# Turning half of a transformer's ternary stages by DMA: six stages on one core, groups 3 to 15 as two 16-bit planes, Gelu in PSUM, second-half tiles among first-half products

## The chip, the core and the metric

The kernel runs on 1 core of one Trainium2 chip. The metric is the device time of one execution in microseconds (us). Three runs of the kernel before the change gave 2587.43, 2589.55 and 2590.55; the median is 2589.55. A difference below about 0.2% (5 us) can't be told from no change.

The engines are named as the profile names them: PE is TensorE (matrix products), PEld its weight loads, DVE is VectorE, ACT is ScalarE, POOL is GpSimd, SP is SyncE, which issues most of the DMAs.

## What is computed

The input x is 8 x 1024 rows of 256 numbers (float32). Six stages follow, each with a residual:

```python
x = x + 0.5 * fp4_ffn(layernorm(x))
x = x + decay_attention(layernorm(x))
x = x + 0.5 * fp4_ffn(layernorm(x))
x = x + 0.5 * ternary_ffn(layernorm(x))
x = x + memory_attention(layernorm(x))
x = x + 0.5 * ternary_ffn(layernorm(x))
```

The change is in the two ternary stages. With W1 (1024 x 256) and W2 (256 x 1024) rounded to -1, 0, 1, one computes

```python
h = gelu(einsum('bsd,fd->bsf', x, ternary(W1)) + b1)
out = einsum('bsf,df->bsd', h, ternary(W2)) + b2
```

## The kernel before

x stays in SBUF for the whole program, as 16 groups `X[g]` of 512 rows: 128 partitions (rows of a tile) x 4 tiles x 256. NG is 16, G is 4 (tiles per group), NF is 8 (blocks of 128 hidden numbers), P is 128, TG is 512.

The program is written in Python through a library that sets all semaphores, hands out buffers and orders each engine's instructions at compile time: it takes the instructions of the text in their order and moves one forward when the earlier ones are not ready by its own model of times. `pin` ties instructions to their written order in other stages; in the ternary stages (`loose`) it does not. A pool with `bufs=n` hands out n buffers per tag in turn, and a buffer is free when all its users are done.

`ffn_ternary` (L1138) runs a loop of 18 turns (L1237). In turn g:

- `norm_turn(g)` (L1168 on) turns the normalized group g from rows to columns. For each of the two halves of the 256 numbers, four 128x128 transposes on TensorE against the identity (L1174) fill a PSUM bank `pt`; ScalarE casts it to a rounded 32-bit type, `xh` (L1177), and VectorE subtracts that from the bank, `xl` (L1179), so that xh + xl carries the full precision through two products.
- `hidden(g - 1)` makes the first half of the feed-forward for the group before: for each f of 8 blocks, four products of 128x512 (L1193) into a PSUM bank `ph`, Gelu on ScalarE from `ph` to the SBUF tile `hf` (L1201), a rounded copy `hh` on ScalarE (L1202), and the remainder `hl` = hf - hh on VectorE (L1204). Behind the first blocks stand the entries of `between`: the normalization of group g + 1 (`norm`, four VectorE operations, L1155), a share of the LayerNorm statistics (`ln.advance`: L235, L236 and small Newton steps L248 to L264), and in the last turns the begin of the next stage. Behind the last four blocks stand the additions of the second bias (`biased`, L1165).
- `down(g - 2)` makes the second half: for each of four tiles, 16 products of 128x256 (L1220) into a bank `po`, and VectorE adds half of it to `X[g]` (L1228). In the last stage the finished group is written to the output by a DMA on SP's queue (L1235; the last group tile by tile, L1233).

PSUM has eight banks here: 2 for `pt`, 4 for `ph`, 2 for `po`. `hf` has four buffers, `hh` and `hl` two each.

How far ahead the statistics are made is a plan (L353): sizes of the pieces in groups, and for each group the turn by which it is due.

The program already turns data by DMA elsewhere: in the fp4 stages a `dma_start_transpose` moves 16-bit grids (L912, L1084), from SP's queue.

Of the kernel before, what the change touches and what calls it, by code (L numbers as in the profile page):

```python
# [9 lines left out]
F32 = mybir.dt.float32  # L10
F32R = mybir.dt.float32r
BF16 = mybir.dt.bfloat16
I32 = mybir.dt.int32
AF = mybir.ActivationFunctionType
ALU = mybir.AluOpType
AX = mybir.AxisListType
PSUM = bass.MemoryType.PSUM

P = 128
D = 256  # L20
# [3 lines left out]
G = 4  # L24
TG = G * P
# [14 lines left out]
def macaron_kernel(  # L40
# [25 lines left out]
    nc = tc.nc  # L66
    NB, S, _ = x.shape
    NG = NB * S // TG
# [16 lines left out]
    out_v = out.rearrange("b s d -> (b s) d").rearrange("(g t p) d -> g p t d", t=G, p=P)  # L85
# [4 lines left out]
    xn_pool = ctx.enter_context(tc.tile_pool(name="xn_pool", bufs=1))  # L90
# [38 lines left out]
    X = []  # L129
    for g in range(NG):  # L130
        xg = xpool.tile([P, G, D], F32, name=f"x_{g}")
        X.append(xg)
        if g == 0:
# [4 lines left out]
                out=A0.lng[:, H : H + 2], in_=gamma_rep.rearrange("(m p) -> p m", p=P)  # L138
# [11 lines left out]
    b1c = w_l1.tile([P, NF], F32, name="b1c")  # L150
# [117 lines left out]
    def statistics(sizes, dues):  # L268
# [81 lines left out]
        "fp4": ((3, 1, 2, 4, 4, 2), [0 if g < 3 else G * (g - 2) + 2 for g in range(NG)]),  # L350

        "decay": ((2, 2, 4, 4, 4), [max(0, G * g - 5) for g in range(NG)]),
        "ternary": ((2, 2, 4, 4, 4), [max(0, g - 1) for g in range(NG)]),  # L353

        "memory": (
            (GB + 3, 3, 4, NG), [max(0, G * (g - GB) - 4) for g in range(NG)]
# [42 lines left out]
    def transpose_group(src, dst, psum, tag, both_act=False, pin=lambda ins: ins):  # L399

        for k in range(2):
            pt = psum.tile([P, TG], F32, tag=tag, name="pt")
            for j in range(G):
                pin(
                    nc.tensor.transpose(
                        pt[:, j * P : (j + 1) * P], src[:, j, k * P : (k + 1) * P], ident
                    )
                )
            if k == 0 or both_act:
                nc.scalar.copy(dst[:, k, :], pt)  # L410
            else:
                pin(nc.vector.tensor_copy(dst[:, k, :], pt))

    def fp4_first(xn, mg, pool):

# [722 lines left out]
    def ffn_ternary(last, after=None):  # L1138
        with ExitStack() as st:
            lnp = st.enter_context(tc.tile_pool(name="f1_ln", bufs=2))  # L1140
            hp = st.enter_context(tc.tile_pool(name="f1_h", bufs=2))
            tp = st.enter_context(tc.tile_pool(name="f1_t", bufs=4))
            ps_t = st.enter_context(tc.tile_pool(name="f1_pt", bufs=2, space=PSUM))
            ps_h = st.enter_context(tc.tile_pool(name="f1_ph", bufs=4, space=PSUM))
            ps_o = st.enter_context(tc.tile_pool(name="f1_po", bufs=2, space=PSUM))
            xns, xts, hs = {}, {}, {}
            ln, xns[0] = begun.pop("ternary")
            loose.append("ternary")

            def norm(g):  # L1150
                xn = xn_pool.tile([P, G, D], F32, tag="xn", name="xn")
                for j in range(G):
                    n = G * g + j
                    pin(
                        nc.vector.tensor_scalar(  # L1155
                            xn[:, j, :], X[g][:, j, :], ln.mv[:, n, 0:1], ln.lr[:, n : n + 1],
                            ALU.subtract, ALU.mult,
                        )
                    )
                xns[g] = xn  # L1160

            def biased(j, g):

                xj = X[g][:, j, :]
                pin(nc.vector.tensor_tensor(xj, xj, b2h, ALU.add))  # L1165

            def norm_turn(g):
                xn = xns.pop(g)  # L1168
                xh = lnp.tile([P, 2, TG], F32R, tag="xh", name="xh")
                xl = lnp.tile([P, 2, TG], F32R, tag="xl", name="xl")  # L1170
                for k in range(2):
                    pt = ps_t.tile([P, TG], F32, tag="pt", name="pt")
                    for j in range(G):
                        nc.tensor.transpose(  # L1174
                            pt[:, j * P : (j + 1) * P], xn[:, j, k * P : (k + 1) * P], ident
                        )
                    nc.scalar.copy(xh[:, k, :], pt)  # L1177
                    pin(
                        nc.vector.tensor_tensor(  # L1179
                            xl[:, k, :], pt, xh[:, k, :].bitcast(F32), ALU.subtract  # L1180
                        )
                    )
                xts[g] = (xh, xl)

            def hidden(g, between):
                xh, xl = xts.pop(g)
                hh = hp.tile([P, NF, TG], F32R, tag="hh", name="hh")
                hl = hp.tile([P, NF, TG], F32R, tag="hl", name="hl")
                for f in range(NF):
                    ph = ps_h.tile([P, TG], F32, tag="ph", name="ph")  # L1190
                    for k in range(2):
                        for xt in (xh, xl):
                            nc.tensor.matmul(  # L1193
                                ph,
                                lhsT=w1[:, k, f * P : (f + 1) * P],
                                rhs=xt[:, k, :],
                                start=(k == 0 and xt is xh),
                                stop=(k == 1 and xt is xl),
                            )
                    hf = tp.tile([P, TG], F32, tag="hf", name="hf")  # L1200
                    nc.scalar.activation(hf, ph, AF.Gelu, bias=b1c[:, f : f + 1])  # L1201
                    nc.scalar.copy(hh[:, f, :], hf)  # L1202
                    pin(
                        nc.vector.tensor_tensor(  # L1204
                            hl[:, f, :], hf, hh[:, f, :].bitcast(F32), ALU.subtract
                        )
                    )
                    if f < len(between):
                        between[f]()
                    elif f >= NF - G:  # L1210
                        biased(f - NF + G, g)
                hs[g] = (hh, hl)

            def down(g):
                hh, hl = hs.pop(g)
                for j in range(G):
                    po = ps_o.tile([P, D], F32, tag="po", name="po")
                    for f in range(NF):
                        for ht in (hh, hl):
                            nc.tensor.matmul(  # L1220
                                po,
                                lhsT=ht[:, f, j * P : (j + 1) * P],
                                rhs=w2[:, f, :],
                                start=(f == 0 and ht is hh),
                                stop=(f == NF - 1 and ht is hl),
                            )
# [7 lines left out]
                if last and g < NG - 1:  # L1234
                    nc.sync.dma_start(out=out_v[g], in_=X[g])  # L1235

            for g in range(NG + 2):  # L1237
                between = []
                if g < NG:
                    norm_turn(g)  # L1240
                    if g + 1 < NG:
                        between.append(lambda: norm(g + 1))
                    between.append(lambda: ln.advance(g))
                    if after and g >= NG - 6:
                        between.append(lambda: begin(after, NG - g))
                if 0 <= g - 1 < NG:
                    hidden(g - 1, between)
                else:
                    for do in between:
                        do()  # L1250
                if 0 <= g - 2 < NG:
                    down(g - 2)
            loose.pop()


# [850 lines left out]
```

## Time and profile before

The profile is of one execution on the chip.

| What | us |
|---|---|
| profiled execution | 2594.43 |
| its span, first to last instruction | 2592.7 |
| median of three runs | 2589.55 |
| first ternary stage, first L1193 to last L1220 | 1491.8 to 1748.4 |
| second ternary stage, the same | 2332.5 to 2589.3 |

The granted TensorE clock is 0.993 over the span and 1.00 in all stretches of the ternary stages.

| Row (line, engine, tile) | count | mean ns of one |
|---|---|---|
| L1174 PE, transposes to pt | 256 | 278 |
| L1193 PE, first half, ph | 1024 | 398 |
| L1220 PE, second half, po | 2048 | 280 |
| L1201 ACT, Gelu | 256 | 695 |
| L1202 ACT, hh | 256 | 628 |
| L1204 DVE, hl | 256 | 684 |
| L1177 ACT, xh | 64 | 590 |
| L1179 DVE, xl | 64 | 680 |
| L1155 DVE, normalization | 120 | 407 |
| L1165 DVE, bias addition | 128 | 415 |
| L1228 DVE, tile addition | 128 | 421 |
| L1486 POOL, 128x1024 addition (another stage) | 16 | 2385 |

How to read it: a TensorE product overlaps the next, so its mean is longer than its share of the time, and distances between starts are used instead. In lists of instructions, "x8" merges eight of a kind, and a bracket at the end tells how long the engine had been idle before the line and what released it. Times in them are us from the span's start.

### The profile page before, as it was taken

How to read it: one execution, taken by the hardware profiler on the slowest of the kernel's cores; microseconds unless marked ns; L12 is line 12 of the kernel's file. 1: busy time of each engine (PE TensorE's matmuls, PEld its weight loads, DVE VectorE, ACT ScalarE, POOL GpSimd, SP SyncE). 2: the span in 40 equal slices, each digit the busy share in tenths (PEclk: the TensorE clock that was granted, in tenths of full speed). 3: DMA queues.
4: the chain of work that ended last, by engine and by line, in shares of the span. 5: the costliest groups of instructions: out<-in, count | busy, mean ns of one | idle time of the engine just before them, and what ended most of it. 6: DMA issues, size and time to landing. Idle time of an engine off the chain costs nothing.

```text
span 2592.7 us, 52415 instructions
## 1 busy us (share of the span) xinstructions
PE 2506.9 (97%) x20426; PEld 1868.6 (72%) x20426; DVE 2087.8 (81%) x4808; ACT 1235.1 (48%) x2785; POOL 900.9 (35%) x895
## 2 busy tenths in 40 slices
PE   4899999999999999999999999999999999999999
PEld 2577777766666666777777689995677776778998
DVE  7898888758878778988888599647888888879864
ACT  5344444334333333444444276656555555437664
POOL 4565555521101003555555300004555555530000
PEclk9899999999999999999999999999999999999999
DMA  7455556500000002556555300000000000000001
GB/s 218 87 117 115 113 118 116 107 23 18 10 22 14 2 2 48 114 116 115 117 116 113 66 1 1 1 1 1 2 2 2 2 2 2 2 2 26 33 33 41
DMA packets 199897, 132.40 MB, mean 51 GB/s; under 512 B 138048, under 2 KB 174944, under 8 KB 199648
## 3 DMA queue, kind: packets, MB, share of 16 engines
q1 hardware_dynamic: 198704, 127.85, 22.8%
q8 instruction: 161, 2.64, 0.4%
q0 software_dynamic: 240, 0.54, 0.1%
q14 instruction: 88, 0.72, 0.1%
q10 hardware_dynamic: 704, 0.66, 0.1%
HBM read 80.77 MB, written 16.52 MB: 38 GB/s over the span
## 4 chain that ended last, share of the span: by engine, by line
PE 84%; DVE 11%; ACT 2%; issue 1%; DMA 1%; POOL 1%; SPq 0%; DVEq 0%; POOLq 0%; ACTq 0%
PE po L960 11%; PE pu L861 10%; PE pg L861 10%; PE po L1220 9%; PE ph L1193 9%; PE sc L1263 5%; PE py L1347 5%; PE pq L1361 4%; PE pkv L1361 4%; PE po L1361 4%; PE pk L1361 4%; PE py L1329 2%; PE pmo L1786 2%; DVE at L1272 1%; DVE qp L804 1%
## 5 line engine op out<-in xcount | busy, mean ns | idle before, releaser
L960 PE MATMUL po<-wd,ht 128*128 128x256 f32 x1536 | 358.1, 383 | 0.6 <-DVE x L969 0.5
L861 PE MATMUL pu<-wgu,xt 128*128 128x352 f32 x1024 | 349.6, 464 | 8.3 <-DVE h L876 7.9
L861 PE MATMUL pg<-wgu,xt 128*128 128x352 f32 x1024 | 348.8, 463 | 4.4 <-ACT sg L871 4.1
L960 PEld LDWEIGHTS po<-wd,ht 128*128 128x128 f32 x1536 | 294.6, 193 | 62.4 <-issue 2.2
L871 ACT ACTIVATE sg<-pg 128x352 f32<-128x352 f32 x256 | 118.1, 461 | 451.5 <-PE pg L861 422.6
L817 POOL TENSOR_TENSOR h<-h,q_rs 128x704 f32<-128x704 f32 (+1 forms) x128 | 176.2, 1376 | 413.1 <-DVE q_rs L811 413.1
L861 PEld LDWEIGHTS pu<-wgu,xt 128*128 128x128 f32 x1024 | 186.5, 193 | 112.3 <-issue 19.6
L861 PEld LDWEIGHTS pg<-wgu,xt 128*128 128x128 f32 x1024 | 195.0, 191 | 97.8 <-ACT sg L871 9.2
L1220 PE MATMUL po<-w,hl 128*128 128x256 f32 x1024 | 243.7, 280 | 1.4 <-DVE hl L1204 1.2
L1220 PE MATMUL po<-w,hh 128*128 128x256 f32 x1024 | 243.3, 280 | 0.0
L1902 POOL TENSOR_TENSOR mo<-mo 128x256 f32<-128x256 f32 x192 | 164.2, 855 | 196.6 <-DVE mo L1799 188.1
L927 POOL TENSOR_TENSOR ht<-gt,ht 128x768 f32<-128x768 bf16 x124 | 205.7, 1659 | 0.0
L1193 PE MATMUL ph<-xh,w 128*128 128x512 f32 x512 | 204.4, 401 | 1.4 <-ACT hf L1201 0.6
L1193 PE MATMUL ph<-xl,w 128*128 128x512 f32 x512 | 201.8, 395 | 0.0
L1204 DVE TENSOR_TENSOR hl<-hf,hh 128x512 fp32r<-128x512 f32 x256 | 168.3, 684 | 39.4 <-ACT hh L1202 35.9
L1220 PEld LDWEIGHTS po<-w,hl 128*128 128x128 f32 x1024 | 192.1, 188 | 4.5 <-DVE hl L1204 2.5
L1220 PEld LDWEIGHTS po<-w,hh 128*128 128x128 f32 x1024 | 192.1, 188 | 2.6 <-DVE x L1228 0.3
L1201 ACT ACTIVATE hf<-ph,b1c 128x512 f32<-128x512 f32 x256 | 168.0, 695 | 18.5 <-PE ph L1193 16.1
L1272 DVE TENSOR_TENSOR at<-sc,dec 128x512 f32<-128x512 f32 x256 | 158.6, 682 | 11.8 <-PE sc L1263 11.8
L886 DVE SCALAR_TENSOR_TENSOR h<-qp,h 128x704 f32<-128x704 f32 x124 | 110.2, 889 | 69.1 <-ACT qp L821 68.9
L1272 DVE TENSOR_TENSOR at<-sc,tri 128x512 f32<-128x512 f32 x256 | 164.9, 679 | 0.4 <-PE sc L1263 0.4
L1202 ACT CAST hh<-hf 128x512 fp32r<-128x512 f32 x256 | 149.2, 628 | 17.0 <-PE po L1220 15.2
(276 smaller groups left out, 5303.0 us busy)
## 6 DMA issues: line engine op xcount, KB each, us to landing
ht<-sd SPq DMA_DIRECT2D x124, 384.0 KB
xt<-sd SPq DMA_DIRECT2D x56, 256.0 KB
sd<-sct SPq DMA_DIRECT2D x124, 64.0 KB
x<-in_x SPq DMA_DIRECT2D x15, 512.0 KB
out<-x SPq DMA_DIRECT2D x15, 512.0 KB
t_raw<-in_w_t SPq DMA_DIRECT2D x16, 256.0 KB
gt<-gd SPq DMA_TRANSPOSE x124
gtx<-xn SPq DMA_TRANSPOSE x56
```

What stands on the lines that cost most here:

```text
L817: pin(mul.tensor_tensor(vb, vb, rs[:, :, None].to_broadcast([P, nb, 16]), ALU.mult))
L861: nc.tensor.matmul(ps, lhsT=xts[g][:, 2 * j + k, :], rhs=wgu[:, k, (2 * q + of_up) * NHALF : (2 * q + of_up + 1) * NHALF], start=(k == 0), ...
L927: nc.gpsimd.tensor_tensor(wide.rearrange("p c t -> p (c t)"), grid.rearrange("p c t -> p (c t)"), wide.rearrange("p c t -> p (c t)"), ALU. ...
L960: nc.tensor.matmul(po, lhsT=ht[:kn, c, :], rhs=wd[:kn, c, :], start=(c == 0), stop=(c == NC - 1),)
L1193: nc.tensor.matmul(ph, lhsT=w1[:, k, f * P : (f + 1) * P], rhs=xt[:, k, :], start=(k == 0 and xt is xh), stop=(k == 1 and xt is xl),)
L1201: nc.scalar.activation(hf, ph, AF.Gelu, bias=b1c[:, f : f + 1])
L1202: nc.scalar.copy(hh[:, f, :], hf)
L1204: nc.vector.tensor_tensor(hl[:, f, :], hf, hh[:, f, :].bitcast(F32), ALU.subtract)
L1220: nc.tensor.matmul(po, lhsT=ht[:, f, j * P : (j + 1) * P], rhs=w2[:, f, :], start=(f == 0 and ht is hh), stop=(f == NF - 1 and ht is hl),)
L1272: nc.vector.tensor_tensor(at, sc.rearrange("p m (e t) -> p (m e) t", e=2), weight, ALU.mult)
L1361: nc.tensor.matmul(dst, lhsT=lhsT, rhs=rhs, start=n == 0, stop=n == len(parts) - 1)
L1902: summed = nc.gpsimd.tensor_tensor(mo[:, :, :, 0, :], mo[:, :, :, 0, :], mo[:, :, :, m, :], ALU.add)
```

## The change

Groups 0 to 2 are turned as before, but their transposes take banks from the `ph` tag. From group 3 on (`by_dma`):

- The normalization is made two groups ahead instead of one. GpSimd then copies the low and the high 16 bits of the 1024 numbers per partition into two planes (`apart`), and one DMA transpose on SP's queue turns both (`turned`).
- In turn g GpSimd joins the planes again, four copies of 512 columns (`xf`); behind one of the first blocks of `hidden(g - 1)` ScalarE casts all 1024 columns to `xh`, and GpSimd makes `xl`.

For all groups, Gelu writes back into `ph`, and `hh` and `hl` read it there; `hf` is gone. `ph` has six banks, `pt` none. The tiles of `down(g - 2)` stand behind blocks 1, 3, 5 and 7 of `hidden(g - 1)`, one each, instead of behind the whole of it. The plan of the statistics has smaller and earlier pieces.

```diff
-        "ternary": ((2, 2, 4, 4, 4), [max(0, g - 1) for g in range(NG)]),
+        "ternary": (
+            (2, 2, 2, 2, 4, 4), [0 if g < 2 else 1 if g == 2 else g - 2 for g in range(NG)]
+        ),
...
+    def planes_turned(xn, pool):
+        words = xn.rearrange("p t d -> p (t d)").bitcast(U16).rearrange("p (n b) -> p n b", b=2)
+        apart = pool.tile([P, 2, G * D], U16, tag="apart", name="apart")
+        for b in range(2):
+            nc.gpsimd.tensor_copy(apart[:, b, :], words[:, :, b])
+        turned = pool.tile([P, 2, 2 * G, P], U16, tag="turned", name="turned")
+        nc.sync.dma_start_transpose(
+            out=turned.rearrange("p b n t -> p (b n) t"),
+            in_=apart.rearrange("p b n -> p (b n)"),
+        )
+        return turned
+
+    def planes_joined(turned, dst):
+        words = dst.rearrange("p k t -> p (k t)").bitcast(U16)
+        words = words.rearrange("p (k j t b) -> p b k j t", k=2, j=G, b=2)
+        for b in range(2):
+            for k in range(2):
+                nc.gpsimd.tensor_copy(
+                    words[:, b, k],
+                    turned[:, b].rearrange("p (j k) t -> p k j t", k=2)[:, k],
+                )
...
-            tp = st.enter_context(tc.tile_pool(name="f1_t", bufs=4))
-            ps_t = st.enter_context(tc.tile_pool(name="f1_pt", bufs=2, space=PSUM))
-            ps_h = st.enter_context(tc.tile_pool(name="f1_ph", bufs=4, space=PSUM))
+            gp = st.enter_context(tc.tile_pool(name="f1_g", bufs=2))
+            ps_h = st.enter_context(tc.tile_pool(name="f1_ph", bufs=6, space=PSUM))
...
+            by_dma = lambda g: g > 2
...
-                xns[g] = xn
+                xns[g] = planes_turned(xn, gp) if by_dma(g) else xn
...
+                if by_dma(g):
+                    xf = gp.tile([P, 2, TG], F32, tag="xf", name="xf", bufs=1)
+                    planes_joined(xn, xf)
+
+                    def split():
+                        nc.scalar.copy(xh, xf)
+                        nc.gpsimd.tensor_tensor(xl, xf, xh.bitcast(F32), ALU.subtract)
+
+                    return split
...
-                    hf = tp.tile([P, TG], F32, tag="hf", name="hf")
-                    nc.scalar.activation(hf, ph, AF.Gelu, bias=b1c[:, f : f + 1])
-                    nc.scalar.copy(hh[:, f, :], hf)
+                    nc.scalar.activation(ph, ph, AF.Gelu, bias=b1c[:, f : f + 1])
+                    nc.scalar.copy(hh[:, f, :], ph)
                     pin(
                         nc.vector.tensor_tensor(
-                            hl[:, f, :], hf, hh[:, f, :].bitcast(F32), ALU.subtract
+                            hl[:, f, :], ph, hh[:, f, :].bitcast(F32), ALU.subtract
                         )
                     )
...
+                    if tiles and f % 2:
+                        tiles.pop(0)()
...
-                    norm_turn(g)
-                    if g + 1 < NG:
-                        between.append(lambda: norm(g + 1))
+                    split = norm_turn(g)
+                    for m in (g + 1, g + 2):
+                        if m < NG and by_dma(m) == (m == g + 2):
+                            between.append(lambda m=m: norm(m))
...
+                    if split:
+                        between.append(split)
+                tiles = down(g - 2) if 0 <= g - 2 < NG else []
                 if 0 <= g - 1 < NG:
-                    hidden(g - 1, between)
+                    hidden(g - 1, between, tiles)
```

More of the change, by code (lines that the diff above doesn't have):

```diff
@@ L13 @@
 I32 = mybir.dt.int32
+U16 = mybir.dt.uint16
 AF = mybir.ActivationFunctionType
@@ L1150, in norm @@
             def norm(g):
-                xn = xn_pool.tile([P, G, D], F32, tag="xn", name="xn")
+                if by_dma(g):
+                    xn = gp.tile([P, G, D], F32, tag="xn", name="xn", bufs=1)
+                else:
+                    xn = xn_pool.tile([P, G, D], F32, tag="xn", name="xn")
                 for j in range(G):
@@ L1170, in norm_turn @@
                 xl = lnp.tile([P, 2, TG], F32R, tag="xl", name="xl")
+                xts[g] = (xh, xl)
+                if by_dma(g):
+                    xf = gp.tile([P, 2, TG], F32, tag="xf", name="xf", bufs=1)
[4 more added lines that the diff above has]
+                    return split
                 for k in range(2):
-                    pt = ps_t.tile([P, TG], F32, tag="pt", name="pt")
+                    pt = ps_h.tile([P, TG], F32, tag="ph", name="pt")
                     for j in range(G):
@@ L1182, in norm_turn, with hidden @@
                     )
-                xts[g] = (xh, xl)
-            def hidden(g, between):
+            def hidden(g, between, tiles):
                 xh, xl = xts.pop(g)
@@ L1215, in down, with one @@
                 hh, hl = hs.pop(g)
-                for j in range(G):
+                def one(j):
                     po = ps_o.tile([P, D], F32, tag="po", name="po")
@@ L1233, in down @@
                         nc.sync.dma_start(out=out_v[g][:, j, :], in_=X[g][:, j, :])
-                if last and g < NG - 1:
-                    nc.sync.dma_start(out=out_v[g], in_=X[g])
+                    elif last and j == G - 1:
+                        nc.sync.dma_start(out=out_v[g], in_=X[g])
+                return [lambda j=j: one(j) for j in range(G)]
             for g in range(NG + 2):
@@ L1245, in ffn_ternary @@
                         between.append(lambda: begin(after, NG - g))
+                    if split:
+                        between.append(split)
+                tiles = down(g - 2) if 0 <= g - 2 < NG else []
                 if 0 <= g - 1 < NG:
-                    hidden(g - 1, between)
[L1248 to L1252, printed above, removed]
+                    hidden(g - 1, between, tiles)
+                for do in tiles if 0 <= g - 1 < NG else between + tiles:
+                    do()
             loose.pop()
```

## The prediction

> **What bounds the kernel now.** I read the engine totals on the first part of the page, then the table of busy time by stretch over the two ternary stages, then the timeline of TensorE across one group, and last the rows of the operations that the change moves.
>
> ```profile
> PE 2506.9 (97%) x20426; PEld 1868.6 (72%) x20426; DVE 2087.8 (81%) x4808; ACT 1235.1 (48%) x2785; POOL 900.9 (35%) x895
> ```
>
> TensorE is the bound, but this is a mean over six stages. The change touches two of them, so their own stretches count (columns: stretch, length, then busy time of PE, PEld, DVE, ACT, POOL, granted clock, DMA share, GB/s):
>
> ```profile
> 1583.00:1599.00 16.00, 16.00 (x108) 14.52 (x107) 15.90 (x56) 10.23 (x18) 0.00 (x0) 1.00 0.00 0
> 1647.00:1663.00 16.00, 16.00 (x107) 14.52 (x106) 10.73 (x23) 10.33 (x19) 0.00 (x0) 1.00 0.00 1
> ```
>
> TensorE has no hole in either. GpSimd and the DMA queues are empty, ScalarE has a third free. VectorE is full in the first row and two thirds full in the second: up to about 1610 it also works off the LayerNorm statistics of all later groups, after that it does a group's own work only. The second ternary stage shows the same two levels (15.9, then 10.8). One group on TensorE:
>
> ```profile
> 1614.51 0.28 PE L1220 MATMUL po<-w,hl 128*128 128x256 f32 x1
> 1614.63 1.03 PE L1174 MATMUL pt<-ident,xn 128*128 128x128 f32 x8
> 1615.42 0.48 PE L1193 MATMUL ph<-xh,w 128*128 128x512 f32 x1
> 1615.74 0.39 PE L1193 MATMUL ph<-xl,w 128*128 128x512 f32 x1
> 1615.97 0.39 PE L1193 MATMUL ph<-xh,w 128*128 128x512 f32 x1
> ```
>
> Durations overlap, so I count from start to start. The eight transposes take 0.79 us (1614.63 to 1615.42), and the first product behind them 0.32 where the others take 0.233. The previous group's first product starts at 1599.54, so a group's period is 15.88: 32 first-half products at 0.233 (7.47), 64 second-half products at 0.1178 (7.53), and 0.88 for the turning.
>
> **What the change removes from the path.** Groups 3 to 15 of both stages, 26 groups, lose their transposes: 26 x 0.88 = 22.9 us, if what remains stays as dense. It takes the period to 15.00.
>
> **Switching between product shapes.** A second-half tile behind every second first-half product makes eight switches a group instead of two. At the start of the first ternary stage the present order mixes them already: from second half to first, the next start comes 0.11 to 0.12 later (1510.90 to 1511.02), the other way 0.23 (1512.64 to 1512.87), which is what each product costs among its like. So 0.
>
> **ScalarE.** Gelu from PSUM to SBUF takes 695 ns (L1201). PSUM to PSUM isn't in the trace; rows of 128x512 that read PSUM or write it lie between 590 (L1177) and 695, so between a gain of 0.8 and nothing per group. The cast L1202 will read PSUM, as L1177 does at 590 against 628. The 1024-wide cast of xh replaces two of 0.59. Of 10.3 busy in 16 it stays near 10 in 15: cost 0, covered by its own idle third.
>
> **GpSimd.** It was idle here and now gets, per group, two plane copies of 1024 columns, four joins of 512 and one subtraction of 1024. The subtraction has its row: 2.39 us (L1486, two inputs, 128x1024). A 16-bit strided copy isn't in the trace. The lower end is its one-input cast of 128 columns, 289 ns, against 198 for one column (L475, L1654): 0.7 to 0.8 ns a column. The upper end is the two-input rate of L1486, 2.33 ns. For the 4096 columns and six fixed parts of 0.19 that is 4.4 or 10.7, with the subtraction 6.8 or 13.1 us a group. I take 6.8: the one-input row is nearer to a copy. Both ends are below 15.0, so GpSimd doesn't set the pace.
>
> **The DMA turning.** One transposing DMA of 128x2048 16-bit values per group. The present 128x768 one (L912) is issued at 315.30 and its packets fill the DMA engines from 316.5 to 317.6: 1.2 us to the first packet and 1.1 for the data. 2048 columns make 1.2 + 2.9 = 4.1 us; if the whole 2.3 scaled, 6.1. It is asked for one period and more ahead (normalized behind a product of the group two back, joined at the start of its own turn), so it is covered by at least 10 us. On SP's queue it stands ahead of the output of group g-2 in the last stage, and that output's wait for VectorE ends within the same group, before the next turning is due. Cost 0; without that cover up to 6 a group.
>
> **VectorE.** It loses the two xl subtractions of 0.68 (1.28 for the pair). A group then needs 10.7 - 1.3 = about 9.5 of 15.0. But GpSimd now works beside it, and there is a price for that in this trace. The same 128x256 normalization takes at most 415 ns in the ternary stages, where GpSimd is idle, and here, at the first of four beside L548 on GpSimd (at 34.2), 1141:
>
> ```profile
> L991 DVE TENSOR_SCALAR xn<-x,ln_mv,ln_r x8: 395/402/1141, 34.2 to 996.5; 128x256 f32<-128x256 f32 x8
> ```
>
> Likewise L396, with both inputs in SBUF, took 1629 ns beside a GpSimd operation and 892 without. By these rows the contenders are the four normalizations, the four bias additions (x, b2h) and some Newton steps, ten a group; the hl subtraction reads PSUM for one input now. GpSimd is busy 6.8 of 15, and what is left of its operation when met is about 0.7 us on a length-weighted mean, so a wait of about 0.3 each: 3 us a group as the likely value, 0 at best, 6.8 (all of GpSimd's time) at worst. 9.5 + 3 = 12.5 is below 15.0: hidden where VectorE has room. The Trainium skill, "SBUF — State Buffer", section "Who interferes with whom", says that a VectorE operation with two SBUF inputs and a GpSimd operation that reads SBUF exclude each other for a whole instruction; by that rule each of eight such meetings could cost up to 2.39 us, 19 a group, and the change would lose; the row above shows 0.74.
>
> **The ring of PSUM banks at the start of a stage.** Here a wait is added. A bank of ph was freed by Gelu (four banks, with four hf buffers behind them) and is now freed by VectorE's hl, six banks in all, and the transposes of groups 0 to 2 take theirs from the same six. In the even part hl ends 2.1 to 3.6 us behind its product, far less than six banks at 1.87 (11 us). At the start VectorE is late:
>
> ```profile
> 1504.45 1.31 PE L1174 MATMUL pt<-ident,xn 128*128 128x128 f32 x8 [0.65 <-DVE xn L1155]
> 1506.71 0.39 PE L1220 MATMUL po<-w,hl 128*128 128x256 f32 x1 [0.95 <-DVE hl L1204]
> ```
>
> From the first product (1491.78) to the last (1748.4) the stage takes 256.8, its work 16 x 15.00 and about 14 x 0.88, 252.3: TensorE loses about 4 us here now, and as much in the second. If the order stayed, the first product of group 1 would want the bank of group 0's third product, whose hl ends at 1506.65, instead of starting at 1501.2: 5.4 later. If VectorE subtracts first and does statistics later, the 4 vanish. So -4 to +5.4 per stage; with some of the 3 us of GpSimd's waits in the full stretch added, I take +3, nearer to the upper end since the statistics are wanted earlier than now (pieces of two groups, due at g-2). Queued behind a late hl on VectorE are only the next hl and the tile additions; TensorE waits for them when six banks are out.
>
> **Sum.** -22.9 + 2 x 3 = -16.9 us. The profiled execution took 2594.43 (span 2592.7), so 2577.5; the median of the runs is 4.9 lower, 2589.55, so 2572.6 for a median. With the ends of the ring (-4 and +5.4 each) 2558.7 to 2577.5.
>
> **Rivals.**
>
> VectorE stays full in the first half of the stages. Between groups 3 and 8 it now shows 15.9 of 16 (the first row). Less 1.3, plus 3 of GpSimd's waits is 17.6 against 15.0: 2.6 a group over six groups, 15.6, of which the ring covers some 8. Each stage loses 7.6 and 2 at its start, 19 in all: 2589.5 - 22.9 + 19.2 = 2586, no change. For it: both engines contend in the only rows that show them together. Against it: the statistics in that stretch are not due, and hl need not stand behind them.
>
> Slower: VectorE blocked by GpSimd everywhere. If each microsecond of GpSimd's work holds VectorE, a group costs 9.5 + 6.8 = 16.3, against 15.88 now: +0.42 x 26 = +11, 2600. With the upper 13.1 it is 22.6 and +175. It decides from 5.5 us of blocking a group (15.0 - 9.5), and is slower than before from 6.4. For it: the 1141. Against: three of those four normalizations and most meetings elsewhere show nothing.
>
> GpSimd too slow: six copies above 2.8 ns a column (15.0 - 2.4 - 1.1 over 4096) make it the bound. At 4 ns, 19.9 a group, +4.0 x 26 = +104, 2694. No row is as slow.
>
> The change doesn't do what it says: the transposes go, and the time returns as gaps between mixed products. 0.1 us at each of the eight switches would eat 0.8 of the 0.88: 2588. The adjacent starts quoted above speak against it.
>
> **Chances.** Forecast 0.70 (2559 to 2578). VectorE full in the first half, in part or whole, 0.14, half of it still faster by over 0.2%. Blocked everywhere 0.09, GpSimd too slow 0.04, gaps 0.03. A difference below 0.2%, 5 us, can't be told from none in this kernel. Faster 0.77, same 0.10, slower 0.13. The range leaves out the slower cases and half of the full-VectorE case: 2559 to 2587.
>
> **What would show it.** Right: starts of neighbouring TensorE products at 0.117 and 0.233 with no L1174 behind group 2, a period of 15.0, the two stages some 9 us shorter each, GpSimd about half busy, DMA packets for 4 us a group. The VectorE rivals would show as first-half products released by hl in groups 3 to 8, or bias additions far above 0.42; a slow GpSimd as xl releasing the first product of each group; the ring as waits in the first 20 us. The forecast is wrong if the period in the even part isn't 15.0.

## The result: slower, 2609.1 us against 2590.1

| | before | changed |
|---|---|---|
| median (range), same chip | 2590.05 us (2587.43 to 2591.08, 4 runs) | 2609.14 us (2603.04 to 2609.27, 4 runs) |
| ratio, 95% interval | | 1.0069 [1.0052, 1.0087] |
| profiled execution, its span | 2594.43, 2592.7 | 2609.17, 2607.5 |
| first ternary stage, first ph product to last po product | 256.5 | 264.7 |
| second ternary stage | 256.7 | 261.1 |
| from the one to the other | 584.2 | 585.8 |

The forecast was 2572.6 us, the upper end of its range 2587. The stages, which should have lost some 8.5 us each, grew by 8.2 and 4.4.

**The profile after, view by view.** Engine totals:

```profile
PE 2495.8 (96%) x20218; PEld 1854.3 (71%) x20218; DVE 2099.4 (81%) x4780; ACT 1243.9 (48%) x2759; POOL 1098.5 (42%) x1077
```

TensorE does 11 us less (208 transposes are gone), GpSimd 198 us more, and VectorE, which lost 52 subtractions xl, some 35 us, is busier by 12 than before. Three stretches of the first stage, each 15 us (columns: stretch, length, busy time of PE, PEld, DVE, ACT, POOL, granted clock, DMA share, GB/s):

```profile
1558.00:1573.00 15.00, 11.73 (x76) 10.42 (x75) 15.00 (x40) 8.35 (x14) 7.64 (x7) 0.99 0.19 36
1594.00:1609.00 15.00, 12.10 (x77) 10.57 (x76) 15.00 (x43) 8.44 (x14) 7.73 (x7) 1.00 0.11 20
1690.00:1705.00 15.00, 15.00 (x97) 13.52 (x97) 6.94 (x13) 10.46 (x18) 5.19 (x6) 1.00 0.00 1
```

In the last row TensorE has no hole, and its starts repeat after 15.01 us: this is the kernel that was forecast. In the first two rows TensorE has holes of three microseconds and VectorE none at all. The table of waits over the first stage names them (engine, line waited for, us in total, times, longest):

```profile
PEld po L1261 <- DVE hl L1242: 13.0, 7, 3.5
PE po L1261 <- DVE hl L1242: 11.4, 6, 3.3
PE pt L1214 <- DVE hl L1242: 2.3, 1, 2.3
```

Second-half products wait for `hl`; first-half products, on which the forecast had looked, are not among them. The ring of banks shows once, in the last row: at 1506 a transpose of group 2 waits for the bank that an `hl` frees. One such hole, on TensorE:

```profile
1569.45 0.28 PE L1261 MATMUL po<-w,hh 128*128 128x256 f32 x1
1573.07 0.58 PE L1261 MATMUL po<-w,hl 128*128 128x256 f32 x1 [3.34 <-DVE hl L1242]
1573.45 0.63 PE L1232 MATMUL ph<-xh,w 128*128 128x512 f32 x1
1573.87 0.63 PE L1232 MATMUL ph<-xl,w 128*128 128x512 f32 x1
```

It is the end of the first tile of group 4's second half: 16 products need all eight blocks of `hh` and `hl`, and the last block's `hl` comes at 1573. VectorE in front of it:

```profile
1563.89 0.69 DVE L1242 TENSOR_TENSOR hl<-ph,hh 128x512 fp32r<-128x512 f32 x1
1564.49 0.42 DVE L1269 SCALAR_TENSOR_TENSOR x<-po,x 128x256 f32<-128x256 f32 x1
1564.83 0.41 DVE L1185 TENSOR_SCALAR xn<-x,ln_mv,ln_r 128x256 f32<-128x256 f32 x1
1565.14 0.24 DVE L237 BATCH_NORM_AGGREGATE ln_mv<-ln_s 128x2 f32<-128x6 f32 x2
1565.31 2.75 DVE L1195 TENSOR_TENSOR x<-x,b2h 128x256 f32<-128x256 f32 x3
1567.98 0.68 DVE L1242 TENSOR_TENSOR hl<-ph,hh 128x512 fp32r<-128x512 f32 x1
1568.58 2.01 DVE L1195 TENSOR_TENSOR x<-x,b2h 128x256 f32<-128x256 f32 x1
1570.51 1.58 DVE L1185 TENSOR_SCALAR xn<-x,ln_mv,ln_r 128x256 f32<-128x256 f32 x2
1572.01 0.40 DVE L1269 SCALAR_TENSOR_TENSOR x<-po,x 128x256 f32<-128x256 f32 x1
1572.34 0.67 DVE L1242 TENSOR_TENSOR hl<-ph,hh 128x512 fp32r<-128x512 f32 x1
```

and GpSimd beside it:

```profile
1565.30 2.48 POOL L422 COPY apart<-xn 128x1024 uint16<-128x1024 uint16 x2 [7.87 <-DVE xn L1185]
1567.74 2.56 POOL L1208 TENSOR_TENSOR xl<-xf,xh 128x1024 fp32r<-128x1024 f32 x1
1570.37 3.00 POOL L436 COPY xf<-turned 128x512 uint16<-128x512 uint16 x4
```

Four bias additions that take 0.42 each when alone take 4.8 together. Taken one by one, two of them end 0.3 behind the two plane copies (1566.9 and 1568.0 against 1566.6 and 1567.8), the fourth 0.3 behind `xl` (1570.6 against 1570.3). And they are group 5's four (counting them from the start of the stage), which the program as written ("the text" from here on) has behind the last blocks of group 5; the normalizations at 1570.51 belong to group 9. All of them run ahead, in front of the last `hl` of group 4, whose last product had started at 1563.82. VectorE never idles there, so its order, set at compile time, has no hole in which a wait could be made good.

The stalls of this kind in groups 4 to 8 of the first stage are 3.50, 1.16, 1.79 + 2.48, 0.31 and 1.06 + 2.42, 12.7 us. After the longer ones comes a second loss. The row of the stretch behind the hole above:

```profile
1573.00:1576.00 3.00, 2.93 (x7) 2.36 (x8) 3.00 (x9) 0.61 (x1) 2.39 (x3) 0.50 0.00 0
```

The granted clock is 0.50, and six to eight first-half products start 0.427 apart instead of 0.233; three times in the stage, with some second-half products behind the third, 5.3 us. Stalls, half clock and the start of the stage (4.5 in its first 35 us; the kernel before loses 3.2 there and nothing behind) make 22.5 of the 23.1 us by which the stage is longer than its products.

### The profile page after: what moved, and what is told of

Its sections match the earlier page's. It is cut to its first block, busy times and chain, and to the rows that moved or that the text cites. A ratio compares the mean times of both kernels' runs of the same rounds, so it can differ in the third digit from the quotient of the medians.

```text
span 2607.5 us, 52298 instructions
## 1 busy us (share of the span) xinstructions
PE 2495.8 (96%) x20218; PEld 1854.3 (71%) x20218; DVE 2099.4 (81%) x4780; ACT 1243.9 (48%) x2759; POOL 1098.5 (42%) x1077
## 5 line engine op out<-in xcount | busy, mean ns | idle before, releaser
L1261 PE MATMUL po<-w,hl 128*128 128x256 f32 x1024 | 251.6, 283 | 20.2 <-DVE hl L1242 20.0
L1242 DVE TENSOR_TENSOR hl<-ph,hh 128x512 fp32r<-128x512 f32 x256 | 174.7, 683 | 101.5 <-ACT hh L1240 100.5
L1261 PE MATMUL po<-w,hh 128*128 128x256 f32 x1024 | 249.2, 282 | 2.1 <-DVE x L1269 2.1
L1239 ACT ACTIVATE ph<-ph,b1c 128x512 f32<-128x512 f32 x256 | 169.9, 668 | 150.3 <-PE ph L1232 150.2
L1261 PEld LDWEIGHTS po<-w,hl 128*128 128x128 f32 x1024 | 194.3, 190 | 28.6 <-DVE hl L1242 22.9
L1232 PE MATMUL ph<-xl,w 128*128 128x512 f32 x512 | 207.4, 405 | 0.0
L1530 POOL TENSOR_TENSOR x<-x,ob 128x1024 f32<-128x1024 f32 x16 | 38.2, 2384 | 341.2 <-ACT xn L318 319.0
```

The lines of the kernel that those rows point to most:

```text
L1232: nc.tensor.matmul(ph, lhsT=w1[:, k, f * P : (f + 1) * P], rhs=xt[:, k, :], start=(k == 0 and xt is xh), stop=(k == 1 and xt is xl),)
L1239: nc.scalar.activation(ph, ph, AF.Gelu, bias=b1c[:, f : f + 1])
L1242: nc.vector.tensor_tensor(hl[:, f, :], ph, hh[:, f, :].bitcast(F32), ALU.subtract)
L1261: nc.tensor.matmul(po, lhsT=ht[:, f, j * P : (j + 1) * P], rhs=w2[:, f, :], start=(f == 0 and ht is hh), stop=(f == NF - 1 and ht is hl),)
```

## Experiments

In the first four expectations theory A is the short way from a group's last `hl` to its second half (5.4 us from the end of the last first-half product to the product that reads this `hl`, 17.5 before the change; the 15.9 written there reaches only to the second half's first product), and theory B the ring of PSUM banks. From the fifth run on A says that VectorE is over-full, and letters are explained where they come up. Every time is a median beside the kernel before on the same chip (2590.2 to 2591.8).

### 1. Without the planes

```diff
-by_dma = lambda g: g > 2
+by_dma = lambda g: False
```

> The changed kernel with no group turned by DMA: all 16 by TensorE, GpSimd idle in the ternary stages; tiles among the first half, Gelu in PSUM, six banks and the new plan stay. Theory A says that the short hand-over costs only because GpSimd holds VectorE up: bias additions back at 0.415 us, hl late by 3.5 us as before, no stall at the first tile beyond group 2, period 15.9, 2586 to 2594. If the mixed order or the plan were the cause by itself, the stalls of groups 4 to 8 stay and the time is above 2605, since the transposes come back.

2596.49 us, ratio 1.0019 [1.0009, 1.0028], 2.5 above the range of theory A; stages 257.0 and 258.1. Behind group 2 no wait of TensorE is left, although the second half stands almost as close behind the first as in the changed kernel (6.2 us against 5.4). The bias additions:

```profile
L1195 DVE TENSOR_TENSOR x<-x,b2h x64: 390/419/431, 1489.6 to 1701.2; 128x256 f32<-128x256 f32 x64
```

(min, median and max in ns.) In the changed kernel the same row reads

```profile
L1195 DVE TENSOR_TENSOR x<-x,b2h x64: 385/417/2536, 1489.8 to 1652.3; 128x256 f32<-128x256 f32 x64
```

So Gelu in PSUM, the six-bank ring, the mixed order and the new plan cost the stages 0.5 and 1.4 us together. The damage comes with GpSimd's work.

### 2. and 3. The tiles elsewhere

All tiles of a second half behind the whole first half:

```diff
-if tiles and f % 2:
-    tiles.pop(0)()
```

> The changed kernel with its four second-half tiles behind the whole first half of the next group, as before the change; planes by DMA and Gelu in PSUM stay. Theory A (hand-over: a tile behind block 1 wants the last hl of the group before some 5.4 us after its product, 15.9 before the change, and VectorE, held up by GpSimd, is 6 to 10 us late in groups 4 to 8): the stalls inside the first tile of a group vanish, period 15.0 from group 3 on, 2565 to 2577 us. Theory B (ring: hl frees the banks now, so TensorE stops wherever hl is late, in any order of tiles; with first-half products in one run, 0.93 us each, six banks cover only 5.6 us): the waits move into the first half, 2595 to 2612.

2616.91 us, 1.0098 [1.0083, 1.0113]; 263.4 and 266.9 us. And the tiles behind the blocks 5, 6 and 7 and after the last:

```diff
-if tiles and f % 2:
+if tiles and f >= 5:
```

> The changed kernel with the tiles behind blocks 5, 6, 7 and one behind the whole, instead of 1, 3, 5, 7: the first tile comes 3.7 us later, so that the last hl of the group before has 9.1 us instead of 5.4. Theory A: the stalls of 3.5, 1.2, 4.4, 0.3 and 3.6 us in the first stage fall to about 1 in all, and with them the stretches of half clock behind them: 2572 to 2586. Theory B: no gain, 2600 or more.

2620.23 us, 1.0108 [1.0093, 1.0123]; 268.2 and 269.2 us. Both refute theory A of these texts; the first is 5 us above the range of theory B, too. With more distance to the second half the lateness comes back through the banks, those of `ph` that an `hl` frees and those of `po` that a tile addition frees. The first of the two kernels has in its waits over the first stage

```profile
PEld ph L1232 <- DVE hl L1242: 11.0, 13, 1.5
PEld po L1259 <- DVE x L1267: 9.2, 9, 2.3
```

in place of the waits of `po` for `hl` shown above. The order on TensorE chooses the door by which the lateness comes in; it doesn't make it.

### 4. The bias in PSUM

```diff
-ps_h = st.enter_context(tc.tile_pool(name="f1_ph", bufs=6, space=PSUM))
+ps_h = st.enter_context(tc.tile_pool(name="f1_ph", bufs=5, space=PSUM))
+ps_b = st.enter_context(tc.tile_pool(name="f1_pb", bufs=1, space=PSUM))
...
+b2p = ps_b.tile([P, D], F32, tag="b2p", name="b2p")
+nc.vector.tensor_copy(b2p, b2h)
...
-pin(nc.vector.tensor_tensor(xj, xj, b2h, ALU.add))
+pin(nc.vector.tensor_tensor(xj, xj, b2p, ALU.add))
```

> The changed kernel with the second bias held in a PSUM bank, so that the bias addition reads one operand in SBUF instead of two; five banks are left for ph. Theory A, with the two-operand additions as the ones that GpSimd holds up (15.9 of the 24.6 us of waits in the first stage): they return to about 0.42 us, hl is late by under 6 us, and most stalls at the first tile go: 2572 to 2595. If GpSimd does not hold up VectorE through operands in SBUF, or five banks are too few, 2605 to 2625.

2585.64 us, 0.9979 [0.9969, 0.9988]: 23.5 us off the changed kernel, and faster than before, with the same work and a bank less. The additions read one input from PSUM now, and none waits:

```profile
L1198 DVE TENSOR_TENSOR x<-x,b2p x64: 378/408/425, 1492.7 to 1642.2; 128x256 f32<-128x256 f32 x64
```

The stages take 254.2 and 248.3; the second is what the forecast needed (256.7 - 8.45). Control, the five banks alone:

```diff
-ps_h = st.enter_context(tc.tile_pool(name="f1_ph", bufs=6, space=PSUM))
+ps_h = st.enter_context(tc.tile_pool(name="f1_ph", bufs=5, space=PSUM))
```

> The changed kernel with five PSUM banks for the first half instead of six and nothing else: the control for the kernel that kept a copy of the bias in the sixth bank. Theory A (VectorE is over-full while it also makes statistics, since its operations wait on GpSimd's; the lateness reaches TensorE through the hand-over or through the ring): one bank less takes 1.87 us of slack out of a ring that already runs short in groups 3 to 8, so 2609 to 2622 us, and the 23.5 us that the bias copy brought are then all the bias's and more. Rival (the bias copy was faster because five banks happen to space the work better): below 2600 us.

2609.92 us, 1.0072 [1.0057, 1.0087], like the changed kernel. The gain is the bias's alone. The time doesn't show the sixth bank, but the start of the stages does: with five the transposes of group 2 wait 3.6 us for an `hl` in the first stage instead of 2.3, and the first 40 us lose 8.7 and 5.8 us instead of 4.5 and 5.4.

### 5. The same additions on GpSimd

```diff
-pin(nc.vector.tensor_tensor(xj, xj, b2h, ALU.add))
+pin(nc.gpsimd.tensor_tensor(xj, xj, b2h, ALU.add))
```

> The changed kernel with the four bias additions of a group on GpSimd instead of VectorE. VectorE loses its only large operation with two inputs in SBUF, 4 x 0.667 = 2.7 us a group; GpSimd gains 4 x about 0.62 (a fourth of the 2.47 us of its 128x1024 subtraction) = 2.5 us, 7.9 to 10.4 of 15.0. Theory A: the stalls of groups 4 to 8 go as with the bias in PSUM, and all six banks stay: 2575 to 2592 us. Rival (GpSimd's total holds VectorE, whatever VectorE does): more GpSimd work holds up normalizations and the accumulation x<-po more, 2600 to 2620 us.

2612.80 us, 1.0084 [1.0069, 1.0099]; 266.4 and 262.7 us. Theory A was wrong: VectorE had 1.7 us a group less to do, and nothing came of it. The rival had the time and the normalizations right, but not the additions `x<-po`, which read PSUM: they took at most 0.43 us, as before. The longer GpSimd work (an addition takes 770 ns there) held the normalizations instead:

```profile
L1185 DVE TENSOR_SCALAR xn<-x,ln_mv,ln_r x60: 391/769/2037, 1491.7 to 1645.5; 128x256 f32<-128x256 f32 x60
```

### 6. Newton's scratch in PSUM too

On top of the bias in PSUM:

```diff
-b2p = ps_b.tile([P, D], F32, tag="b2p", name="b2p")
+both = ps_b.tile([P, 512], F32, tag="b2p", name="b2p")
+b2p = both[:, 0:D]
...
+scratch.append(both[:, D : D + 64])
```

> The kernel with the bias copied to PSUM, and with the scratch values of the Newton steps in the same bank. Theory A (every VectorE operation with two inputs in SBUF is held by GpSimd): the Newton steps, up to 2.1 us there, fall back to some 0.15 us, worth the last two stalls of 1.7 and 1.4 us in the first ternary stage and their half clock: 2577 to 2586 us. Rival (normalizations with two per-partition operands, up to 2.3 us, are held too, and they make the last stalls): no change, 2583 to 2589 us.

2585.72 us, 0.9982 [0.9973, 0.9991]: no change, the rival's case. The Newton steps fell to at most 0.18 us (ln_r), and the normalizations were held up to 2.55 us.

### 7. GpSimd's longest operation in pieces

```diff
-nc.gpsimd.tensor_tensor(xl, xf, xh.bitcast(F32), ALU.subtract)
+for k in range(2):
+    for c in range(0, TG, P):
+        s = slice(c, c + P)
+        nc.gpsimd.tensor_tensor(
+            xl[:, k, s], xf[:, k, s], xh[:, k, s].bitcast(F32), ALU.subtract
+        )
```

> The changed kernel with GpSimd's subtraction xl in eight pieces of 128 columns (8 x about 0.31 us) instead of one of 2.47 us; GpSimd's work is otherwise the same. If an operation of VectorE waits for the whole GpSimd instruction that it meets, the longest waits (2.1 us over the 0.42 of a bias addition) fall to about 0.3 to 0.7 us, the mean bias addition from 0.667 to about 0.5 us, and the time to 2592 to 2604 us. Rival (the wait is a share of GpSimd's busy time, however it is cut): no change, 2605 to 2614 us, or more by the fixed cost of eight instructions.

2596.90 us, 1.0019 [1.0010, 1.0029], though GpSimd's eight pieces take 0.50 each, 4.0 instead of 2.47. Additions and pieces in its first stage:

```profile
L1195 DVE TENSOR_TENSOR x<-x,b2h x64: 381/413/1254, 1490.7 to 1647.5; 128x256 f32<-128x256 f32 x64
L1211 POOL TENSOR_TENSOR xl<-xf,xh x104: 450/463/805, 1520.2 to 1717.1; 128x128 fp32r<-128x128 f32 x104
```

The longest addition takes 1.25 us, 0.84 of it waiting where 0.3 to 0.7 was expected, and 2.1 in the changed kernel. More GpSimd work, less waiting, 12 us won: what VectorE waits for is the rest of an instruction, not a share of the time.

### 8. Without the statistics

```diff
-n = G * g + j
+n = G * (g % 2) + j
-between.append(lambda: ln.advance(g))
```

> The changed kernel without the statistics of groups 2 to 15 in both ternary stages (their means and scales are taken from groups 0 and 1, so what is normalized differs); GpSimd's and TensorE's work is as in the changed kernel. Theory A (it takes the statistics and the waits on GpSimd together to over-fill VectorE in groups 3 to 8): the stalls of groups 4 to 8 go, both stages fall to some 16 x 15.0 + 9 = 249 us as the even part has it, 2609 - (264.7 - 249) - (261.1 - 249) = 2581 us, range 2574 to 2590. Rival (one long wait of one bias addition behind GpSimd is enough to make a block late, whatever else VectorE does): stalls stay in groups 3 to 8 and appear in none other, 2600 to 2610 us.

2600.43 us, 1.0036 [1.0024, 1.0047]; 264.3 and 257.2 us. Mostly the rival's outcome: the first stage kept its stalls, 3.93 and 1.44 at the first of them. VectorE in front of that one:

```profile
1534.65 0.68 DVE L1242 TENSOR_TENSOR hl<-ph,hh 128x512 fp32r<-128x512 f32 x1
1535.25 0.41 DVE L1269 SCALAR_TENSOR_TENSOR x<-po,x 128x256 f32<-128x256 f32 x1
1535.58 0.41 DVE L1195 TENSOR_TENSOR x<-x,b2h 128x256 f32<-128x256 f32 x1
1535.91 4.79 DVE L1185 TENSOR_SCALAR xn<-x,ln_mv,ln_r 128x256 f32<-128x256 f32 x4
1540.62 0.67 DVE L1242 TENSOR_TENSOR hl<-ph,hh 128x512 fp32r<-128x512 f32 x1
```

Four normalizations (1.6 us alone) take 4.8 in front of an `hl`, and the four before them had run at 1531.85, four microseconds earlier; the text has one such set per group, 15 us apart. Taking work away doesn't make room: the compiler moves other later work forward into it. That gave theory C.

### 9. VectorE in the order of the text

The ternary stages are no longer `loose`, so that `pin` holds VectorE to the written order; and since a turn's statistics would then stand in one lump, they are dealt out over the eight blocks:

```diff
-loose.append("ternary")
...
+for share in shares[f * len(shares) // NF : (f + 1) * len(shares) // NF]:
+    share()
...
-between.append(lambda: ln.advance(g))
+if g == 0:
+    between.append(lambda: ln.advance(g))
...
-loose.pop()
```

> The changed kernel with VectorE's order in the ternary stages held to the order of the source, with the statistics of a group dealt out over its eight blocks; in the changed kernel the compiler lets statistics, normalizations and bias additions of later groups run ahead of a block's hl (the bias of group 10 stood in front of the first hl of group 7). The waits on GpSimd remain. Theory C (what makes a block late is that run-ahead work stands in front of its hl in a queue that is thereby full until the work has run out, as it was also without the statistics; a wait on GpSimd has then no room to be made good): the stalls of groups 4 to 8 shrink to the single waits, 16 x 15.0 + 9 to 14 = 249 to 254 us a stage, 2578 to 2594 us. Rival D (the single waits, and a queue that in source order stops at each x<-po until its tile is done, are enough): stalls in all groups, 2600 us or more.

2592.46 us, 1.0004 [0.9995, 1.0013]; 254.8 and 254.0 us: 16.7 us off the changed kernel, theory C's case. A stretch in the middle of the first stage, where the changed kernel had 12.10 busy of 15 (second row of its stretches above):

```profile
1594.00:1609.00 15.00, 15.00 (x98) 13.52 (x97) 13.27 (x31) 10.46 (x18) 7.50 (x7) 1.00 0.19 37
```

The sharpest point is that VectorE waits for GpSimd no less than in the changed kernel: 26.2 us in each stage against 24.4 and 21.4 (the excess of every bias addition, normalization and Newton step over its mean before the change). The waits are there; what is gone is the run-ahead work that stood with them in front of `hl`. Behind the first 40 us of a stage TensorE loses 2.7 and 1.7 us to holes and half clock here, in the changed kernel 18.6 and 14.2. The edit has two parts, and the dealing out of the statistics was not run alone; but with no statistics at all (run 8) the compiler's order still loses 19.7 and 12.6 there. The same order together with the bias in PSUM (run 4):

```diff
-loose.append("ternary")
...
-pin(nc.vector.tensor_tensor(xj, xj, b2h, ALU.add))
+pin(nc.vector.tensor_tensor(xj, xj, b2p, ALU.add))
...
```

> The same order of VectorE, and the bias in PSUM (one bank less for the first half). Theory C: hardly a wait is left and none of it meets run-ahead work: 248 to 252 us a stage, 2575 to 2588 us, at or below the 2585.6 us of the bias copy alone. Rival D (source order costs by itself, since each x<-po stops the queue): slower than the bias copy alone, 2590 us or more.

2588.61 us, 0.9988 [0.9979, 0.9998]; 253.1 and 252.7 us. At the edge between the two: no better than the bias copy in the compiler's order, so the written order has a price of its own. In the changed kernel it lies at the start: in their first 40 us the stages lose 10.5 and 10.7 us in the written order and 10.2 each with the bias in PSUM as well, against 4.5 and 5.4, and 9.0 and 6.7 with that bias, in the compiler's order. Nor are the waits gone here, as theory C had it: some 18 us a stage are left, in normalizations and Newton steps. The kernel before in the written order, statistics dealt out as above:

```diff
-loose.append("ternary")
...
```

> The kernel before, with VectorE's order in the ternary stages held to the order of the source and the statistics dealt out over the blocks, and nothing of the change: the control for the same order on the changed kernel, which took 16.7 us off. If that gain is the removal of run-ahead work from in front of hl where waits on GpSimd make it late, nothing is won here, since the period is TensorE's 15.88 us and the hand-over has 14 us: 256 to 259 us a stage, 2588 to 2600 us. Rival (the compiler's order is bad by itself, for both kernels): 2572 to 2584 us.

2619.56 us, 1.0111 [1.0097, 1.0125]; 273.8 and 266.6 us, worse than either case expected. The order isn't better by itself, far from it:

```profile
DVE x L1230 <- PE po L1222: 59.8, 34, 3.3
```

VectorE stands still 60 us in the first stage because each tile addition stops the queue until its tile is done. The changed kernel, with its tiles among the first half's products, bears the written order; the kernel before does not.

### 10. Bias in PSUM and pieces together

```diff
...
-pin(nc.vector.tensor_tensor(xj, xj, b2h, ALU.add))
+pin(nc.vector.tensor_tensor(xj, xj, b2p, ALU.add))
...
-nc.gpsimd.tensor_tensor(xl, xf, xh.bitcast(F32), ALU.subtract)
...
+        nc.gpsimd.tensor_tensor(
+            xl[:, k, s], xf[:, k, s], xh[:, k, s].bitcast(F32), ALU.subtract
+        )
```

> The two edits that each took waits on GpSimd away, together: the bias in PSUM (2585.6 us alone) and the subtraction xl in eight pieces (2596.9 us alone); VectorE's order is left to the compiler as in the changed kernel. If both act on the same lateness, and what is left is each normalization's and Newton step's wait (0.50 us against 0.407; up to 2.3 us), the pieces cut these to at most 0.9 us and both stages come to the 248.3 us that the second one has with the bias copy alone: 2585.6 - (254.2 - 248.3) = 2580 us, range 2574 to 2585. Rival (the pieces' fixed cost, 8 x 0.50 us instead of 2.47, makes GpSimd's products later and eats it): 2585 to 2592 us.

2582.80 us (7 runs), 0.9970 [0.9959, 0.9981], the fastest of all, 8.2 us below the kernel before. The stages take 251.9 and 248.8.

| kernel | waits of VectorE on GpSimd, us per stage | stages, us | median, us |
|---|---|---|---|
| before | 0, 0 | 256.5, 256.7 | 2590 |
| changed | 24.4, 21.4 | 264.7, 261.1 | 2609.1 |
| xl in pieces | 15.5, 15.3 | 258.0, 258.3 | 2596.9 |
| bias in PSUM | 9.4, 7.8 | 254.2, 248.3 | 2585.6 |
| both | 5.8, 5.8 | 251.9, 248.8 | 2582.8 |
| written order | 26.2, 26.2 | 254.8, 254.0 | 2592.5 |

Waits and stages are those of the one profiled execution of each kernel, which took 2587.6 us in the written order, 4.9 below its median, and 2600.6 with xl in pieces, 3.7 above. In the compiler's order time goes with the waits; in the written order it doesn't. Of the 16.9 us that the forecast had, the stages of the last combination show 12.5; 4.7 are given back between them (588.9 us against 584.2), 2.8 of that in the first 40 us of the memory stage. Why that stage begins later there was not followed up. What its ternary stages still lose, 10.3 and 7.2 us, lies mostly in their first 40 us (7.9 and 6.8), where in the first stage the same transposes wait 3.6 us for the bank.

## Why the prediction was wrong

- **Transposes, -22.9.** Right where nothing disturbs: the period of groups 10 to 15 is 15.01 us, with no hole.
- **Mixing product shapes, 0.** Right: without the planes the stages are 0.5 and 1.4 us longer than before, everything else of the change included.
- **ScalarE, 0.** Right. Gelu into PSUM 668 ns, the cast from it 593, the wide xh 1048; 10.46 busy of 15.
- **GpSimd, 6.8 us a group.** 7.9 (two copies at 1.08, four at 0.83, xl 2.47), inside its bounds; far below 15.0, so no bound, as said.
- **DMA, 4.1 us, hidden.** One issued at 1665.1 has its packets between 1666 and 1669 (DMA share 0.91 there, nothing in the two microseconds before and behind): at most 3.9 us. No wait of TensorE for xh or xl stands in the table of waits of either stage.
- **VectorE's waits, 3 us a group.** 24.4 us over 13 groups is 1.9, fewer than taken; but the waits end with group 9, and in the first stage they are 3.2 a group from group 3 to there, about the likely value. The size was right; the failed step is the sentence behind them, "9.5 + 3 = 12.5 is below 15.0: hidden where VectorE has room", with its defence in the rival on a full VectorE, "the statistics in that stretch are not due, and hl need not stand behind them". `hl` does stand behind them. The order on each engine is set at compile time, and the compiler fills every hole with later work that is ready; a queue that is filled in this way has no room, whatever its mean load would allow, and a wait that its planner doesn't know goes straight onto the next `hl`. The row 15.90 of 16.00 had shown that; I read as spare what was spent ahead. Runs 8 and 9 showed it: without the statistics other work filled the queue, and with the written order the same waits cost 17 us less.
- **The ring, +3 a stage.** At its place a small loss: TensorE stopped there once in each stage, 2.5 and 1.75 us, and the first 35 us cost 4.5 and 5.4 us against 3.2 and 3.6 before, so +1.3 and +1.8. (For the kernel before the prediction had a loss of about 4; it counts 14 turnings as work, but 120 transposes, 15 turnings, lie in the stage.) The large loss came elsewhere. I followed a late `hl` to the banks only (11 us of cover). It also feeds the second half, where the change had moved the product that needs the last `hl` from 17.5 to 5.4 us behind the last first-half product; in the even part 2.2 us of it are spare. Every stall from group 4 on came there. But that hand-over isn't the cause either: given more distance (runs 2 and 3), the lateness reached TensorE through the banks.
- **What had no term.** The half clock behind long stalls: 5.3 us in the first stage.
- **The rivals.** "VectorE stays full in the first half of the stages" named the place, groups 3 to 8, and the engine. It priced the case at 2586 because it took 8 us of cover a stage from the ring; with the 2.2 that were spare, its own sum gives 2589.5 - 22.9 + 2 x (15.6 - 2.2 + 2) = 2597, on the slow side. "Blocked everywhere" is refuted by groups 10 to 15.

The sum by terms: the stages grew by 12.6 us where 16.9 were to go, 29.5 apart; 2.2 are outside them; and 4.9 come from the step from the profiled execution to the median, which was 4.9 before and nothing after. Together 36.6; the difference from 2572.6 is 36.5.

## What to carry to other kernels

An engine whose order a compiler fills ahead and that shows 100% busy may hold nothing but work done early, and yet it has no slack: before giving a neighbour work that can hold it up, look at what stands in its queue in front of the result that the bound engine wants next. When an operation moves to an idle engine, ask whose operations it can hold up there, and where their operands lie; here one bias tile copied to PSUM was worth 23.5 us. And follow a late result to all its readers, the one that the change has moved closer first.

## What the runs showed of the hardware

- Beside GpSimd, a VectorE addition of two SBUF inputs (415 ns alone) took up to 2536 ns, and with one of them in PSUM at most 425. The Trainium skill, "SBUF — State Buffer", section "Who interferes with whom", says that such an operation and a GpSimd operation that reads SBUF shut each other out for a whole instruction. The prediction set that rule against a row of 0.74 us; runs 4 and 7 agree with the rule.
- Normalizations, with one SBUF tensor and two per-partition values, are held as well: 407 ns alone, up to 2.04 us in run 5 and 2.55 in run 6.
- The half clock (0.50) followed every stall of TensorE of 2.52 us or more (from start to start, beyond the usual distance) in the ternary stages of these kernels, shorter ones when another stood close by (1.79 and 2.48, with a few products between), and of lone ones from 2.0 to 2.5 some (1.98 without the planes, 2.22 in the five-bank kernel) and not others (2.30 with all tiles behind, 2.50 at the start of the changed kernel's first stage). The Trainium skill, "TensorE: Matmul & The Clock Gate", in its section "Why this matters for your kernels", asks for no idle gap above about 3 us; here some 2.0 were enough at times.
- A strided 16-bit copy on GpSimd took on the mean 1.08 us for 1024 columns and, into every second half-word, 0.83 for 512; a subtraction of 128 columns 0.46 to 0.50 against 2.40 to 2.47 for 1024.
